# Cached keys of later groups turned by VectorE and moved by DMAs that ScalarE issues; the first sequence's tokens held twice

## The chip, the core and the metric

The kernel runs on one core of a Trainium2 chip. The core has a matrix engine (PE, with its weight loads shown as PEld), a vector engine (DVE), an activation engine (ACT), a general engine (POOL) and a queue engine that only issues transfers (SP). The metric is the device time of one execution in microseconds: before the change a median of 3047.43 us over 3 runs (3047.22 to 3047.49).

## The reference

A decoder layer with the norm after each of its three blocks. `x` has 32 sequences of 64 tokens with 512 features, 2048 token rows in all.

```
x = layernorm(x + attn(x))         # 32 heads, 8 key/value groups, head size 128
x = layernorm(x + xattn(x, ctx))   # the same heads over a context of 64 tokens a sequence
x = layernorm(x + ffn(x))          # one 512 x 512 product and a low-rank correction
```

The change lies in the first block:

```
q, k, v = x @ wq.T, x @ wk.T, x @ wv.T
q, k    = apply_rope(q), apply_rope(k)            # one position for all tokens
k_full  = concatenate([k_cache[block_idx], k[0]]) # 512 cached keys, 64 of the first sequence
v_full  = concatenate([v_cache[block_idx], v[0]])
out     = softmax(q @ k_full.T / sqrt(128)) @ v_full;  attn = out @ wo.T
```

All 2048 tokens attend to the same 576 keys, of which the first sequence gives 64. The kernel doesn't rotate the queries: since one rotation holds for all, it turns the cached keys back by it instead, and scales the new keys.

## The kernel before

**Stages.** Three stages follow each other: the self-attention (about the first 1840 us), the keys and values of the context (some 200 us), and the cross-attention with the feed-forward block. Everything is in 32-bit floating point.

**Units.** The first stage runs over 128 units: 8 groups (`NKV`) of 16 units, a unit being one head (4 a group, `REP`) with one block of 512 tokens (4 blocks, `NTB`). Unit r of a group, r = 0 to 15, is block r // 4, head r % 4. In a unit, `scores` runs four times, for 128 tokens each: two matmuls of 288 keys into `s` (two buffers), the row maximum on DVE (`nmax`), the exponential on ACT into `p`, the division on DVE, and a transpose of 32 x 32 blocks on DVE (`turn`) into `T` (two buffers). `move` then brings `T` to the tile `pT` (two buffers, each for two units) by 16 transfers that SP issues. Two units later `values` multiplies `pT` by the values on PE: those of unit n run in unit n + 2, the first of them after the second `scores`. Between the scores stand the products of the queries (`q_`) and of the output projection (`w_`).

**Order.** In this stage the program writes the order on PE, DVE and ACT by hand; SP's order and POOL's come from a scheduler. All engines work through their own list in order. A unit takes 12 to 18 us.

**Keys.** While a group runs, the keys of the next are made in steps:
- r = 4, 5, 6, 8: `gather_keys` and `gather_values` fetch 128 cached rows each by indirect transfers from POOL into `kn` and `v`.
- r = 8: `new_keys` multiplies the tokens of the first sequence (`x64`, 64 columns) by the weights of the group. The keys (`pk`) come out turned already, as head features x tokens. The values (`pv`) are wanted on partitions 0 to 63 and once more on 64 to 127, so each of the four parts of the 512 features has two matmuls with the same 64 columns as stationary operand and different output halves. Both go into the bank `po1`; ACT evicts them into `kT` and `v`.
- r = 9: `rotate` turns the cached keys back on DVE (4 instructions) and POOL (2), from `kn` into `kr`.
- r = 10: `cached_keys` transposes `kr` on PE, four times 128 x 128 into the bank `po1`; ACT evicts it into `kT` in two instructions, which multiply by `SCALE`.

The first group's keys are made in the same way ahead of the first unit.

**Queues and counters.** Every plain transfer of the program, of SP as of ACT, has one of eight completion counters (DMAHW0 to 7), dealt out in the order in which the scheduler placed the transfers. A transfer is issued only when the earlier one on its counter has landed: the issuing engine waits for that, whatever the two transfers carry. SP issues the moves of `T`, the weights `wq` and `wo` and the token blocks `xT`; ACT issues 16 loads of `acc`, a pair `wk`, `wv` for each later group, and a few moves at the stage's two ends. At the end of r = 11 SP issues the four loads of the next group's `wq` and a block `xT` of 1 MB, ahead of that unit's 16 moves.

Lines that are spoken of: 312 all products of queries and projection, 559 the gathers, 594 to 598 `rotate`, 612 and 618 `new_keys`, 622 and 626 its evictions, 632 and 635 `cached_keys`, 651 scores, 656 maximum, 659 exponential, 677 `turn`, 689 `move`, 697 `values`, 110 and 230 the loads of `xT` and of weights, 552 those of `wk` and `wv`, 1127 the cross-attention's transpose on DVE.

Of the kernel before, what the change touches and what calls it, by code (L numbers as in the profile page):

```python
# [9 lines left out]
F32 = mybir.dt.float32  # L10
I32 = mybir.dt.int32
AF = mybir.ActivationFunctionType
ALU = mybir.AluOpType
# [3 lines left out]
P = 128  # L17
DIM = 512
NH, NKV, HD = 32, 8, 128
REP = NH // NKV  # L20
NT = 2048
SEQ = 64
TB = 512
NTB = NT // TB
TPB = TB // P
NC = DIM // P
# [5 lines left out]
SQ = 32  # L32
NQD = P // SQ
# [10 lines left out]
SHARED, NPC = 4, 9  # L44
# [4 lines left out]
SCALE = 1.0 / math.sqrt(HD)  # L49
# [3 lines left out]
def decoder_layer(  # L53
# [30 lines left out]
    nc = tc.nc  # L84
# [412 lines left out]
    later = []  # L497


    with ExitStack() as ph:  # L500
        kv = ph.enter_context(tc.tile_pool(name="kv", bufs=2))
        kc = ph.enter_context(tc.tile_pool(name="kc", bufs=1))
# [11 lines left out]
        NKT = NSEL // P  # L514
        blk = kc.tile([P, NKT], I32, name="blk")
        nc.sync.dma_start(out=blk, in_=block_idx)
        xTs = {0: token_room(0, "xT0")}
# [6 lines left out]
        cs = kc.tile([P, HD // 2], F32, name="cs")  # L524
        sn = kc.tile([P, HD // 2], F32, name="sn")
# [20 lines left out]
        rows_cur, kn_cur, kr_cur, wkv_cur, kTs, vs = {}, {}, {}, {}, {}, {}  # L546
# [51 lines left out]
            nc.vector.tensor_tensor(k4[:, :, :, 0], k4[:, :, :, 0], tmp, ALU.add)  # L598


        x64 = kc.tile([P, NC, SEQ], F32, name="x64")

        def new_keys(g):

            wk, wv = wkv_cur.pop(g)
            kTs[g] = kv.tile([P, NKEY], F32, tag="kT", name=f"kT{g}")
            new = bank([P, 1, TB], f"new{g}", "po1")[:, 0, :]
            pk, pv = new[:, :SEQ], new[:, P : 2 * P]  # L610
            for c in range(NC):
                nc.tensor.matmul(
                    pk, wk[:, c, :], x64[:, c, :], start=(c == 0), stop=(c == NC - 1),
                    skip_group_check=True,
                )
            for c in range(NC):
                for i in range(2):
                    nc.tensor.matmul(
                        pv[i * SEQ : (i + 1) * SEQ, :], x64[:, c, :], wv[:, c, :],
                        start=False, stop=(c == NC - 1), skip_group_check=True,  # L620
                    )
            nc.scalar.activation(
                kTs[g].rearrange("p (s b k) -> p s b k", s=2, k=SQ)[:, :, SHARED, :],
                pk.rearrange("p (s k) -> p s k", s=2), AF.Copy, scale=nrm2,
            )
            nc.scalar.copy(vs[g][:, NKT, :], pv)

        def cached_keys(g, tag="po1"):
            kr = kr_cur.pop(g)
            pt = bank([P, NKT, P], f"pkt{g}", tag)  # L630
            for t in range(NKT):
                nc.tensor.transpose(pt[:, t, :], kr[:, t, :], ident)
            dst = kTs[g].rearrange("p (s b k) -> p s b k", s=2, k=SQ)
            for r0, b0 in ((0, 0), (2, SHARED + 1)):
                nc.scalar.activation(
                    dst[:, :, b0 : b0 + NKT, :],
                    pt[:, :, r0 * SQ : (r0 + 2) * SQ].rearrange("p t (s k) -> p s t k", s=2),
                    AF.Copy, scale=SCALE,
                )

        units = [(g, tb, h) for g in range(NKV) for tb in range(NTB) for h in range(REP)]
        qTs, Ts, pTs, oTs, pos, ps_ = {}, {}, {}, {}, {}, {}

        def scores(n, i):


            g, tb, h = units[n]
            u = f"{g}_{tb}_{h}_{i}"
            s = sc.tile([P, 2, 512], F32, tag="sc", name=f"s{u}")
            for a in range(2):  # L650
                nc.tensor.matmul(  # L651
                    s[:, a, :HALF], qTs[n // REP][:, units[n][2], i * P : (i + 1) * P],
                    kTs[g][:, a * HALF : (a + 1) * HALF], start=True, stop=True,
                )
            nmax = small.tile([P, 1], F32, tag="nmax", name=f"nmax{u}")
            nc.vector.tensor_reduce(nmax, s[:, :, :HALF], AX.XY, ALU.max, negate=True)  # L656
            p = sb.tile([P, NKEY], F32, tag="p", name=f"p{u}", bufs=4)
            den = small.tile([P, 1], F32, tag="den", name=f"den{u}")
            nc.scalar.activation(  # L659
                p.rearrange("q (a k) -> q a k", a=2), s[:, :, :HALF], AF.Exp,  # L660
                bias=nmax, accum_out=den,
            )
            if i == 0:
                Ts[n] = sb.tile([P, NBK, TPB, SQ], F32, tag="T", name=f"T{g}_{tb}_{h}")
                flush()
            else:
                turn(n, i - 1)
            nc.vector.reciprocal(den, den)  # L668
            nc.vector.tensor_scalar(p, p, den, None, ALU.mult)  # L669
            ps_[n, i] = p  # L670
            if i == TPB - 1:
                turn(n, i)
# [123 lines left out]
        t = {i: big.tile([P, 2, HF], F32, tag=f"tx{i}", name=f"tx0_{i}") for i in range(1, 5)}  # L796
        for j in range(NKT):
            gather_keys(0, j)
        nc.gpsimd.tensor_copy(
            x64.rearrange("p c (j k) -> p c j k", j=TPB),  # L800
            xTs[0].rearrange("p c (j k) -> p c j k", j=TPB)[:, :, :, : SEQ // TPB],
        )
        nc.vector.tensor_tensor(t[1], q[0, 1], q[0, 0], sub)
        nc.vector.tensor_tensor(wq0[7], wq0[1], wq0[5], sub)
        nc.vector.tensor_tensor(wq0[5], wq0[5], wq0[4], ALU.add)
# [13 lines left out]
        c = first.c  # L819
# [9 lines left out]
        for j in range(NKT):  # L829
            gather_values(0, j)  # L830
        cached_keys(0, "s0")
        nc.vector.tensor_tensor(t[3], q[1, 1], q[0, 1], sub)
        nc.vector.tensor_tensor(t[4], q[1, 0], t[2], sub)
        tok[1] = token_sums(xTs[1], "tx1", nc.gpsimd)
# [27 lines left out]
        for n in range(N):  # L862
            b, h = divmod(n, REP)
            g, r = units[n][0], n % PER
            if r == REP and g + 1 < NKV:
                load_group(g + 1)
            if r in gathers and g + 1 < NKV:
                gather_keys(g + 1, gathers[r])
            if 0 < n <= PER:


                b2, j = divmod(n - 1, TPB)
                nc.scalar.dma_start(out=acc[b2][:, j, :], in_=rows(x, b2)[:, j, :])
            if r == 2 * REP and g + 1 < NKV:
                later.append(lambda g=g: new_keys(g + 1))
            if r == 2 * REP + 1 and g + 1 < NKV:
                rotate(g + 1)
                later.append(lambda g=g: cached_keys(g + 1))
            if n == N - REP:
                encT[0] = big.tile([P, NC, TB], F32, tag="qT", name="encT0", bufs=2)  # L880
                load_features(encT[0], encT_in, 0)
            steps = {0: "qwqw", 1: "qw q", 2: "wqwq", 3: "w qw"}[h]

            def step(place):
                if n < REP:

                    i = {(0, 0): 3, (0, 1): 7, (0, 3): 4}.get((n, place))
                    if i:
                        last_products(i)
                    elif (n, place) in ((0, 2), (1, 0), (1, 1), (1, 2), (1, 3), (2, 0), (2, 2)):  # L890
                        q_step(n)
                elif steps[place] == "q":
                    q_step(n)
                elif steps[place] == "w":
                    w_step(b - 2 if h < 2 else b - 1)
                flush()

            def spare_bank():

                if n % 2 == 0 and later:  # L900
                    later.pop(0)()

            scores(n, 0)
            step(0)
            spare_bank()
            scores(n, 1)
            if n - 1 in short:
                move(n - 1, (3,), nc.scalar)
            if n >= 2:
                values(n - 2, 0, 2 if n % 2 == 0 else 3)  # L910
            step(1)
            scores(n, 2)
            step(2)
            if r in gathers and g + 1 < NKV:
                gather_values(g + 1, gathers[r])
            scores(n, 3)
            if n >= 2:
                values(n - 2, 2 if n % 2 == 0 else 3, NKT)
                if n % 2:
                    shared_values(n - 2)  # L920
            step(3)
            spare_bank()
            if h == REP - 1:
                if b + 2 < NB:
                    g2, tb2, _ = units[(b + 2) * REP]
                    if tb2 == 0:
                        wq_cur[g2] = load_left(wqT[:, columns(g2)], f"wq{g2}", nc.gpsimd)
                    tok[b + 2] = token_sums(xTs.pop(b + 2), f"tx{g2}_{tb2}", nc.gpsimd)
                elif b + 2 == NB:
                    kvw[0] = load_kv_left(0, "wq")  # L930
                else:
                    encR[0] = token_sums(encT[0], "te0", nc.gpsimd)
            if h == REP - 1 and b + 3 < NB or n == 0:

                b2 = b + 3 if n else 2
                xTs[b2] = token_room(b2, f"xT{b2}")
                load_features(xTs[b2], xT_in, b2 % NTB)
            move(n, (0, 1, 2) if n in short else range(NQD))
# [512 lines left out]
```

## Time and profile before

The profiled execution took 3049.76 us by the device's own count; the span from its first to its last instruction is 3048.0 us. Busy times by stage, in us:

| stretch, us | PE | DVE | ACT | POOL | DMA share |
|---|---|---|---|---|---|
| 0 to 1840 (self-attention) | 1823.22 | 1418.08 | 538.49 | 487.17 | 0.46 |
| 1840 to 2040 (context) | 198.13 | 93.88 | 33.72 | 41.63 | 0.44 |
| 2040 to 3048 (cross-attention, feed-forward) | 993.04 | 688.15 | 211.57 | 418.11 | 0.19 |
| the span, 3048 | 3014.40 | 2200.11 | 783.78 | 946.90 | |

The granted clock of the matrix engine is 0.997 on the mean. The DMA share is the mean busy share of the core's 16 DMA engines. A row of the timeline gives the start, the length, the engine (with q: its queue), the line, the operation, what it writes and reads, and the count of instructions that were merged; in brackets the idle time of the engine ahead of it and what ended that. A matmul in 32 bits shows as two PE records, a transpose as one. In the view of waits a row names who waited, for what, the sum, the number of times and the longest. SP has no busy time: all it does is to wait and to issue.

### The profile page before, as it was taken

What the parts mean: (1) busy time and instruction counts of PE and PEld (TensorE: products, weight loads), DVE (VectorE), ACT (ScalarE), POOL (GpSimd) and SP (SyncE); (2) the same over time, 40 slices, a digit from 0 to 9 for tenths busy, and PEclk for the clock granted to TensorE, in tenths of its full rate; (3) what the DMA queues carried; (4) which work ended last, traced back from release to release, by engine and by line L of the source; (5) the groups of instructions that cost most, each with busy time, mean ns of one, the idle gap of its engine ahead of it and who ended that gap; (6) DMA issues with size and microseconds to landing.
All of it is one profiled execution on the core that took longest, in us unless ns stands there. A gap on an engine that the chain in (4) does not pass through costs nothing.

```text
span 3048.0 us, 42453 instructions
## 1 busy us (share of the span) xinstructions
PE 3014.4 (99%) x14848; PEld 2321.9 (76%) x14848; DVE 2200.1 (72%) x4069; ACT 783.8 (26%) x1892; POOL 946.9 (31%) x774
## 2 busy tenths in 40 slices
PE   8999999999999999999999999999999999999998
PEld 6677777777777777777777768998888888888875
DVE  7777787777777777777877763546666666666787
ACT  2323223223222222222332221111111111111233
POOL 4231321321321321321321223035544444444420
PEclk9999999999999999999999999999999999999999
DMA  5444444444444444444444354351121121121121
GB/s 171 129 130 129 110 115 126 109 113 126 108 114 129 105 121 124 108 123 119 106 126 108 87 133 141 115 160 56 49 63 56 49 65 55 50 67 52 52 61 42
DMA packets 214931, 304.97 MB, mean 100 GB/s; under 512 B 45888, under 2 KB 108864, under 8 KB 214720
## 3 DMA queue, kind: packets, MB, share of 16 engines
q1 hardware_dynamic: 200048, 286.90, 34.7%
q10 hardware_dynamic: 12624, 11.16, 1.3%
q0 software_dynamic: 2048, 4.20, 0.5%
q8 instruction: 120, 1.97, 0.3%
q14 instruction: 91, 0.75, 0.1%
HBM read 107.05 MB, written 20.97 MB: 42 GB/s over the span
## 4 chain that ended last, share of the span: by engine, by line
PE 94%; DVE 2%; SPq 1%; DMA 1%; issue 1%; ACT 1%; POOL 0%; ACTq 0%; DVEq 0%; POOLq 0%
PE po L697 16%; PE s L651 15%; PE sx L1091 2%; PE pox L1163 2%; PE w_2y L312 1%; PE q_3y L312 1%; PE w_0y L312 1%; PE w_3y L312 1%; PE q_2y L312 1%; PE qx_0y L312 1%; PE wx_0y L312 1%; PE wx_3y L312 1%; PE qx_2y L312 1%; PE qx_1y L312 1%; PE wx_1y L312 1%; PE w_1y L312 1%
## 5 line engine op out<-in xcount | busy, mean ns | idle before, releaser
L659 ACT ACTIVATE p<-s,nmax 128x576 f32<-128x576 f32 x512 | 379.1, 740 | 1250.0 <-DVE nmax L656 1233.2
L651 PE MATMUL s<-kT,qT 128*128 128x288 f32 x2048 | 578.0, 408 | 4.9 <-ACT p L659 4.2
L697 PE MATMUL po<-pT,v 128*128 128x512 f32 (+1 forms) x1280 | 552.7, 605 | 6.2 <-DMA pT<-T 4.5
L651 PEld LDWEIGHTS s<-kT,qT 128*128 128x128 f32 x2048 | 388.4, 191 | 108.2 <-issue 19.7
L656 DVE TENSOR_REDUCE nmax<-s 128x1 f32<-128x576 f32 x512 | 384.0, 750 | 62.9 <-PE s L651 62.9
L677 DVE STREAM_TRANSPOSE T<-p 128x576 f32<-128x576 f32 x512 | 394.1, 770 | 4.4
L697 PEld LDWEIGHTS po<-pT,v 128*128 128x128 f32 (+1 forms) x1280 | 214.4, 190 | 208.5 <-issue 182.3
L669 DVE TENSOR_SCALAR p<-p,den 128x576 f32<-128x576 f32 x512 | 316.1, 617 | 17.9
L668 DVE RECIPROCAL den<-den 128x1 f32<-128x1 f32 x512 | 83.9, 164 | 230.9 <-ACT p L659 221.3
L283 POOL TENSOR_TENSOR so<-oT,oT 128x512 f32<-128x512 f32 x32 | 40.7, 1272 | 551.2 <-ACT oT L720 533.9
L286 POOL TENSOR_TENSOR so<-oT 128x512 f32<-128x512 f32 x32 | 40.6, 1270 | 351.2 <-ACT oT L720 100.6
L283 POOL TENSOR_TENSOR sox<-oTx,oTx 128x512 f32<-128x512 f32 x32 | 40.5, 1266 | 296.8 <-ACT oTx L1182 216.0
L1182 ACT ACTIVATE oTx<-pox,bv 128x128 f32<-128x128 f32 x256 | 73.7, 486 | 117.6 <-PE pox L1163 117.6
L224 POOL TENSOR_TENSOR tx<-xT 128x512 f32<-128x512 f32 x31 | 39.6, 1278 | 206.2 <-PE q_3z L312 65.0
L659 ACT ACTIVATION_READ_ACCUMULATOR p<-s,nmax 128x1 f32 x512 | 98.7, 193 | 0.0
L1292 POOL TENSOR_TENSOR txx<-x1T 128x512 f32<-128x512 f32 x31 | 39.3, 1268 | 174.6 <-PE qx_3z L312 75.2
L1108 ACT ACTIVATE ex<-ex 128x512 f32<-128x512 f32 x64 | 40.4, 631 | 201.7 <-DVE ex L1107 201.7
L1184 DVE TENSOR_SCALAR oTx<-pox,bv 128x128 f32<-128x128 f32 x256 | 72.6, 422 | 8.5 <-PE pox L1163 8.5
L1091 PEld LDWEIGHTS sx<-kvx,qTx 128*64 128x64 f32 x2048 | 62.3, 138 | 10.6 <-issue 10.6
L720 ACT COPY oT<-po 128x512 f32<-128x512 f32 x128 | 68.3, 587 | 4.7 <-PE po L697 3.8
L1091 PE MATMUL sx<-kvx,qTx 128*64 128x64 f32 x2048 | 66.7, 224 | 0.0
L1163 PE MATMUL pox<-pTx,kvx 64*128 64x256 f32 x512 | 64.6, 389 | 0.7 <-DMA pTx<-Tx 0.7
(443 smaller groups left out, 5746.1 us busy)
## 6 DMA issues: line engine op xcount, KB each, us to landing
pT<-T SPq DMA_DIRECT2D x1016, 80.0 KB
pT<-T SPq DMA_DIRECT2D x1008, 64.0 KB
xT<-in_xT SPq DMA_DIRECT2D x31, 1024.0 KB
kvx<-kv SPq DMA_DIRECT2D x32, 512.0 KB
pTx<-Tx SPq DMA_DIRECT2D x256, 64.0 KB
kv<-c SPq DMA_DIRECT2D x30, 512.0 KB
wo<-in_woT SPq DMA_DIRECT2D x32, 256.0 KB
xwq<-in_xwq SPq DMA_DIRECT2D x32, 256.0 KB
```

The costliest lines, as they stand in the source:

```text
L283: nc.gpsimd.tensor_tensor(t[1], a[1, 0], a[1, 1], ALU.add)
L312: nc.tensor.matmul(self.banks[b][:, m, :], self.left[i][:, k, m * P : (m + 1) * P], self.right[i][:, k, :], start=(first and m + k == 0), ...
L651: nc.tensor.matmul(s[:, a, :HALF], qTs[n // REP][:, units[n][2], i * P : (i + 1) * P], kTs[g][:, a * HALF : (a + 1) * HALF], start=True, s ...
L656: nc.vector.tensor_reduce(nmax, s[:, :, :HALF], AX.XY, ALU.max, negate=True)
L659: nc.scalar.activation(p.rearrange("q (a k) -> q a k", a=2), s[:, :, :HALF], AF.Exp, bias=nmax, accum_out=den,)
L668: nc.vector.reciprocal(den, den)
L669: nc.vector.tensor_scalar(p, p, den, None, ALU.mult)
L677: nc.vector.transpose(Ts[n][:, :, i, :], ps_.pop((n, i)).rearrange("q (b k) -> q b k", k=SQ))
L697: nc.tensor.matmul(pos[n].rearrange("d (a q) -> d a q", a=NQD), vs[units[n][0]][rows, v, :], pTs[n // 2][rows, :, chunk, :], skip_group_ch ...
L1091: nc.tensor.matmul(s[b * SEQ : (b + 1) * SEQ, i * REP + h, :], qTs[n][:, h, pr * HF + c0 : pr * HF + c0 + SEQ], kvs[n][:, pr, 0, c0 : c0 + ...
L1163: nc.tensor.matmul(po[pr, b][:, i, :].rearrange("d (h a j) -> d h a j", h=REP, a=2), kvs[n][r, pr, 1, i * HD : (i + 1) * HD], pTs[n][r, :, ...
L1182: nc.scalar.activation(dst, src, AF.Identity, bias=bias)
```

## The change

Three edits:
- `x64` becomes the first half of `x128`, which holds the 64 tokens twice. POOL fills it by two copies in place of one. `new_keys` makes the values by one matmul for each part of the features, with 128 stationary columns, in place of two with 64.
- For the seven later groups `cached_keys` (r = 10) goes: four transposes on PE and two evictions on ACT. In its place `turn_keys` follows `rotate` in r = 9: one 32 x 32-block transpose on DVE of 128 x 512, from `kr` back into `kn`. Sixteen transfers of `kn` into `kT`, of 16 KB each in 128 pieces of 128 bytes, carry the blocks to their partitions. ACT issues them, one behind each exponential, in r = 10 to 13. The built program deals them counters of the same eight; the lists of SP and of POOL keep their order, apart from POOL's second copy.
- `SCALE` is no longer applied by the evictions; after the first group's keys, DVE multiplies the cosines and sines (`cs`, `sn`, 128 x 64 each) by it once.

```diff
-        x64 = kc.tile([P, NC, SEQ], F32, name="x64")
+        x128 = kc.tile([P, NC, 2 * SEQ], F32, name="x128")
+        x64 = x128[:, :, :SEQ]
...
             for c in range(NC):
-                for i in range(2):
-                    nc.tensor.matmul(
-                        pv[i * SEQ : (i + 1) * SEQ, :], x64[:, c, :], wv[:, c, :],
-                        start=False, stop=(c == NC - 1), skip_group_check=True,
-                    )
+                nc.tensor.matmul(
+                    pv, x128[:, c, :], wv[:, c, :],
+                    start=False, stop=(c == NC - 1), skip_group_check=True,
+                )
...
+        def turn_keys(g):
+
+            kn_cur[g] = kn_cur[g].rearrange("p t (r k) -> p t r k", k=SQ)
+            nc.vector.transpose(
+                kn_cur[g], kr_cur.pop(g).rearrange("p t (r k) -> p t r k", k=SQ)
+            )
+
+        def move_keys(g):
+
+
+            dst = kTs[g].rearrange("p (s b k) -> p s b k", s=2, k=SQ)
+            for a in range(NQD):
+                b0 = SHARED + 1 if a > 1 else 0
+                for r in range(NQD):
+                    key_moves.append(lambda a=a, b0=b0, r=r: nc.scalar.dma_start(
+                        out=dst[r * SQ : (r + 1) * SQ, a % 2, b0 : b0 + NKT, :],
+                        in_=kn_cur[g][a * SQ : (a + 1) * SQ, :, r, :],
+                    ))
+
+        key_moves = []
...
                 bias=nmax, accum_out=den,
             )
+            if key_moves:
+                key_moves.pop(0)()
...
-        nc.gpsimd.tensor_copy(
-            x64.rearrange("p c (j k) -> p c j k", j=TPB),
-            xTs[0].rearrange("p c (j k) -> p c j k", j=TPB)[:, :, :, : SEQ // TPB],
-        )
+        for i in range(2):
+            nc.gpsimd.tensor_copy(
+                x128[:, :, i * SEQ : (i + 1) * SEQ].rearrange("p c (j k) -> p c j k", j=TPB),
+                xTs[0].rearrange("p c (j k) -> p c j k", j=TPB)[:, :, :, : SEQ // TPB],
+            )
...
         cached_keys(0, "s0")
+
+        for w in (cs, sn):
+            nc.vector.tensor_scalar(w, w, SCALE, None, ALU.mult)
...
                 rotate(g + 1)
-                later.append(lambda g=g: cached_keys(g + 1))
+                turn_keys(g + 1)
+            if r == 2 * REP + 2 and g + 1 < NKV:
+                move_keys(g + 1)
```

## The prediction

> **What bounds the kernel now.** I read the engines' busy shares and the chain of waits first.
>
> ```profile
> PE 3014.4 (99%) x14848; PEld 2321.9 (76%) x14848; DVE 2200.1 (72%) x4069; ACT 783.8 (26%) x1892; POOL 946.9 (31%) x774
> PE 94%; DVE 2%; SPq 1%; DMA 1%; issue 1%; ACT 1%; POOL 0%; ACTq 0%; DVEq 0%; POOLq 0%
> ```
>
> PE sets the time: a microsecond taken from its list is gained, one that it waits is lost. The timeline of PE shows what the two edited steps take of it, here for the last group:
>
> ```profile
> 1483.16 1.00 PE L612 MATMUL new<-x,wk 128*128 128x64 f32 x8
> 1484.10 1.09 PE L618 MATMUL new<-wv,x 128*64 128x128 f32 x16
> 1485.12 1.24 PE L651 MATMUL s<-kT,qT 128*128 128x288 f32 x4
> ...
> 1513.19 0.60 PE L632 MATMUL pkt<-ident,kr 128*128 128x128 f32 x4
> 1513.63 1.14 PE L651 MATMUL s<-kT,qT 128*128 128x288 f32 x4
> ```
>
> From start to next start, the values of the new keys hold PE for 1.02 us, the transposes for 0.44.
>
> The change puts transfers on ACT, so I then asked what SP's moves wait for, from 150 to 1600 us:
>
> ```profile
> SPq L689 <- DVE T L677: 267.2, 81, 5.8
> SPq L689 <- DMA wk<-in_wkT: 33.5, 6, 5.9
> SPq L689 <- DMA xT<-in_xT: 23.1, 9, 4.2
> SPq L689 <- DMA acc<-in_x: 7.4, 2, 5.0
> ```
>
> The first row is the data. The others are loads that have nothing to do with `pT`; `wk` and `acc` are issued by ACT. That is the shared counter at work: a transfer of ACT holds SP for up to 5.9 us.
>
> Whether PE feels it depends on the slack of `pT`. SP's and PE's timelines at the end of r = 11 in the last group, and PE's rows at the same place in the first and the third group:
>
> ```profile
> 1525.83 10.53 SPq L689 DMA_DIRECT2D pT<-T  x16
> 1536.40 2.15 SPq L230 DMA_DIRECT2D wq<-in_wqT  x4
> 1538.65 0.41 SPq L110 DMA_DIRECT2D xT<-in_xT  x1
> 1539.15 23.86 SPq L689 DMA_DIRECT2D pT<-T  x29
> ...
> 1556.79 2.74 PE L697 MATMUL po<-pT,v 128*128 128x512 f32 x6
> ...
> 197.78 2.81 PE L697 MATMUL po<-pT,v 128*128 128x512 f32 x6 [0.64 <-DMA pT<-T]
> ...
> 651.41 2.81 PE L697 MATMUL po<-pT,v 128*128 128x512 f32 x6 [0.44 <-issue]
> ```
>
> SP runs without a gap from the moves of r = 10 (1525.83) through `wq` and `xT` to those of r = 11. By the trace's landing records `xT` is in at 1548.05, the last move of r = 11 at 1555.15, and PE takes them up at 1556.79. In the seven groups this distance is 0.5, 1.4, 0.3, 2.1, 1.5, 0.3 and 1.6 us; some 0.3 of it is the way from landing to matmul, and in two groups PE already waits. In r = 9, 10 and 12 it is 3.3 us or more. So the values that run in r = 13 are the tight place.
>
> **The change part by part.**
>
> *Transposes off PE.* Seven groups x 0.44 = 3.1 us gained. ACT loses two evictions (0.66 us a group), which nothing waited for but the next group.
>
> *Values by the whole array.* Of the 16 records of line 618 each is 64 ns behind the last (1.02 / 16); 128 columns with a full weight load run at 110 ns (0.44 / 4 in the transposes). Eight such: 0.88 us, a gain of 0.14 a group, 1.0 us for the seven later ones. Here a rule speaks against the edit: the Trainium skill, "TensorEngine Tiling (Array Packing)", section "Theoretical Speedup", lets operands of 64 columns run as two tiles at up to twice the speed. If the halves ran fully beside each other, 0.88 us before, the edit would bring nothing; one after the other (16 x 110 ns = 1.76) it would bring 0.88 a group. The row lies near the first end, and I take it. In the first group the weight loads of the transposes that follow wait 0.17 us for POOL's last rotation, so most of it is lost there.
>
> *DVE's transpose in r = 9.* No such row in this stage; the nearest is the 128x512 transpose of line 1127, 694 ns. It stands ahead of the unit's first maximum (1499.56), delays it by 0.7 us and waits for POOL's last rotation (1498.12 + 0.79 = 1498.91), which DVE's own (1499.22 + 0.42) outlasts. The fourth scores need the second exponential, over at 1504.09, and start at about 1505.69 (1504.72 + 0.97): 1.6 us of cover. Cost 0; with the cover gone 7 x 0.7 = 4.9.
>
> *Scaling of cosines and sines, second copy.* Two small instructions on DVE before 19 us, while it then waits for the first scores until 20.94; POOL's second copy (0.89) ends at 10.6, its next instruction starts at 11.81 on gathered keys. Cost 0.
>
> *ACT's sixteen transfers.* Issuing one from SBUF to SBUF takes ACT some 0.6 us (its moves at line 689: 601 ns). ACT sits idle for 1.2 us or more ahead of every exponential in these units of the last group: hidden. ACT's own counters: I matched each wait in the built program's list with the landing before the change. Two to four moves a group wait for another move of the same set, long landed; nearly all others for a transfer of SP that landed 3 to 10 us earlier. The exception is the third move in r = 12, whose counter belongs to a move queued behind `xT`: from 1.9 us before to 1.4 after the exponential's end. Delayed by SP's 2 us (below) it can hold ACT past the next exponential by a microsecond or two; the second scores of r = 13 need that one 3 us later. Cost 0, up to 2 x 7 = 14 if this cover fails.
>
> *SP behind ACT's transfers.* In r = 11, SP's eleventh or so move has the counter of ACT's second. In the last group the second exponential ends at 1531.78; issue 0.1 later and 2.1 us to land (moves of SP land 2.0 to 2.2 us after issue; pieces of 128 bytes aren't in the trace of before: bounds 1.9, nothing faster being there, and 3.0, the gathers' median) gives 1533.98. SP would have issued at 1532.60: held by 1.4 us, and `wq`, `xT` and the moves of r = 11 with it. Then, behind `xT`: before, the eighth move waits for its counter and nine are left to issue. With ACT's transfers dealt in between, it is the seventh: one more issue, 0.63 us. Per group, in us:
>
> | group | 1 | 2 | 3 | 4 | 5 | 6 | 7 |
> |---|---|---|---|---|---|---|---|
> | SP held in r = 11 | 2.6 | 1.9 | 0.7 | 1.9 | 1.7 | 1.9 | 1.4 |
> | with the extra issue | 3.2 | 2.5 | 1.3 | 2.5 | 2.3 | 2.5 | 2.0 |
> | slack less 0.3 | 0.2 | 1.1 | 0 | 1.8 | 1.2 | 0 | 1.3 |
> | PE waits longer by | 3.0 | 1.4 | 1.3 | 0.7 | 1.1 | 2.5 | 0.7 |
>
> Sum 10.7 us; with a landing of 1.9 it is 9.3, with 3.0 it is 17. In r = 11 to 13 SP is held besides by up to 2 us a unit, which r = 10 and 12 cover with 3.3 us or more.
>
> The second rule to weigh: the Trainium skill, "DMA: Bandwidth & Descriptors", section "Issuing engines are not separate DMA queues", says that issuing from several engines saves only the issuing engine's time. By it the issue on ACT spares SP 16 x 0.63 = 10 us a group and costs it nothing: stall 0, sum -4.1. Below nothing it can't go, since these transfers come on top of SP's. The rows of `wk` and `acc` show a loss all the same, not of bandwidth (DMA share 0.46) but of order; I go by them.
>
> Sum: -3.1 - 1.0 + 10.7 = +6.6, rounded to +7 since the first group's `wq` loads are held as well. Against the profiled execution, 3049.76 + 7 = 3056.8; it lies 2.3 above the median of the runs, so 3047.43 + 7 = **3054.5 us** is my forecast.
>
> **Rivals.**
> 1. *The holds stay hidden* (0.28). If SP makes up what it loses before r = 13, only PE's 4.1 us count: 3043.3. For it: SP idles 4 to 5 us ahead of the moves of r = 8, 9 and 10. Against: no idle time from 1525.83 to `xT`. This case isn't slower.
> 2. *ACT is held too* (0.15). The third move of r = 12 delays exponentials, PE runs out of scores: +7 from above and half of the 14: 3061.5. It decides once such a wait ends over 3 us behind its exponential.
> 3. *The halves ran one after the other* (0.07), with the holds hidden: 7 x (0.44 + 0.88) = 9.2 gained, 3038.2. Against it stands 64 ns a record.
>
> My own case has 0.50. A difference under 0.2% (6.1 us) is about what this measurement can tell from no change. The main case spreads from +3 to +14, mostly above 6.1: 0.40 slower, 0.10 within. With rival 2 slower has 0.55; rival 1 adds 0.27 within and 0.01 faster, rival 3 0.07 faster: within 0.37, faster 0.08. Range for eight in ten: 3042.5 (rival 1 with a little more) to 3063 (a landing of 3.0, or ACT held).
>
> **What would show it.** In the changed profile: lines 632 and 635 only at the start; line 619 taking 0.88 us; SP's waits listing `kT<-kn` some ten times a group; PE's idle time before line 720 (the values) with some 11 us more, in r = 13. If that idle time stays near 6 us, rival 1 holds. If PE's scores wait for ACT, rival 2. If line 619 takes 0.5 us, the rate of 110 ns was wrong.

## The result, and the profile after

The changed kernel takes 3066.19 us, the median of 6 runs (3061.64 to 3068.97), the kernel before beside it 3047.32 (3045.55 to 3049.19, 6 runs). The ratio is 1.0063, with a 95% interval of 1.0053 to 1.0073: **slower by 18.9 us**. The profiled execution took 3064.98 us, 15.2 more than the profiled one of before; the one of before lies 2.4 us above its median beside it, the one of after 1.2 below.

The page of the changed kernel: PE's busy time, the chain of waits, and the group of the values (busy time and mean ns, then PE's idle time ahead of it and what ended most of that), with the last row of before under it.

```profile
PE 3013.8 (98%) x14756; PEld 2319.0 (76%) x14756; DVE 2200.5 (72%) x4078; ACT 778.7 (25%) x1878; POOL 947.2 (31%) x775
...
PE 88%; DVE 4%; DMA 3%; SPq 3%; ACT 1%; issue 1%; POOL 0%; ACTq 0%; DVEq 0%; POOLq 0%
...
L720 PE MATMUL po<-pT,v 128*128 128x512 f32 (+1 forms) x1280 | 553.6, 606 | 16.1 <-DMA pT<-T 15.7
```
```profile
L697 PE MATMUL po<-pT,v 128*128 128x512 f32 (+1 forms) x1280 | 552.7, 605 | 6.2 <-DMA pT<-T 4.5
```

PE's list is shorter by 92 matmuls, yet it is busy for only 0.6 us less, and the chain leaves it far more often (88% for 94). The idle time ahead of the values grew from 6.2 to 16.1 us. From 150 to 1620 us, SP's waits, then PE's, then PE's of before (who waits for what: sum, times, longest):

```profile
SPq L712 <- DMA kT<-kn: 49.1, 21, 7.6
...
SPq L712 <- DMA xT<-in_xT: 4.6, 5, 2.1
...
SPq L230 <- DMA acc<-in_x: 2.7, 1, 2.7
```
```profile
PE po L720 <- DMA pT<-T: 11.1, 6, 2.3
PE q_0x L312 <- DMA wq<-in_wqT: 4.9, 6, 2.8
```
```profile
PE po L697 <- DMA pT<-T: 0.6, 1, 0.6
PE q_0x L312 <- DMA wq<-in_wqT: 0.2, 1, 0.2
```

SP now stands 49 us behind moves of keys, which it has no use for. Where: the queue of SP and the timeline of ACT at the end of r = 11 and in r = 12 of the last group.

```profile
1552.44 2.15 SPq L230 DMA_DIRECT2D wq<-in_wqT  x4
1554.69 0.41 SPq L110 DMA_DIRECT2D xT<-in_xT  x1
```
```profile
1556.28 0.74 ACT L680 ACTIVATE p<-s,nmax 128x576 f32<-128x576 f32 x1 [2.62 <-DVE nmax L677]
1556.33 0.60 ACTq L656 DMA_DIRECT2D kT<-kn  x1
...
1559.35 0.59 ACTq L656 DMA_DIRECT2D kT<-kn  x1
```

Two things are to be read here. ACT issues a move 0.05 us after the exponential ahead of it has begun, not after it has ended. And the two moves of 1556.33 and 1559.35 go out while the 1 MB of `xT` is in flight. By the landing records `xT` is in at 1563.39, the two moves at 1564.2 and 1564.4, 7.9 and 5.0 us after their issue (in groups 2 to 7: 7.9 to 9.1 and 4.8 to 6.1), where the moves of r = 10 and 11 take 2.0 in the median. SP's fourth move of r = 11 has the counter of the first of them. From 1555 to 1580 us SP's waits are one row; under it the row of before for the same place (1539 to 1564 us):

```profile
SPq L712 <- DMA kT<-kn: 6.0, 1, 6.0
```
```profile
SPq L689 <- DMA xT<-in_xT: 3.2, 1, 3.2
```

Before, the eighth move of r = 11 was the first to wait, for `xT` itself, and nine were left to issue once it was in; now it is the fourth, and thirteen are left. In r = 13 PE waits for these moves before it can take up the values: in each of groups 2 to 7, by 1.35 to 2.27 us.

A wait can cost more than its own length. PE's timeline at two such waits, in the sixth group and in the third, and the windows around the first (busy us of PE, PEld, DVE, ACT and POOL, then the granted clock, the DMA share and GB/s):

```profile
1344.82 4.51 PE L720 MATMUL po<-pT,v 128*128 128x512 f32 x6 [2.07 <-DMA pT<-T]
```
```profile
659.46 2.84 PE L720 MATMUL po<-pT,v 128*128 128x512 f32 x6 [2.27 <-DMA pT<-T]
```
```profile
1340.00:1345.00 5.00, 2.93 (x14) 2.19 (x13) 2.80 (x6) 1.66 (x4) 0.00 (x0) 1.00 0.51 122
1345.00:1350.00 5.00, 5.00 (x10) 2.38 (x10) 1.25 (x3) 0.00 (x0) 0.00 (x0) 0.66 0.51 121
```

Behind the first the granted clock is 0.66 in the mean of 5 us and the same six records take 4.51 us, not 2.84. Behind the second, though it is the longer wait, they take no longer.

### The profile page after: what moved, and what is told of

Its sections match the earlier page's. It is cut to its first block, busy times and chain, and to the rows that moved or that the text cites. A ratio compares the mean times of both kernels' runs of the same rounds, so it can differ in the third digit from the quotient of the medians.

```text
span 3063.2 us, 42403 instructions
## 1 busy us (share of the span) xinstructions
PE 3013.8 (98%) x14756; PEld 2319.0 (76%) x14756; DVE 2200.5 (72%) x4078; ACT 778.7 (25%) x1878; POOL 947.2 (31%) x775
## 4 chain that ended last, share of the span: by engine, by line
PE 88%; DVE 4%; DMA 3%; SPq 3%; ACT 1%; issue 1%; POOL 0%; ACTq 0%; DVEq 0%; POOLq 0%
PE po L720 15%; PE s L672 14%; SPq L712 2%; PE sx L1120 2%; PE pox L1192 2%; DMA kT<-kn 2%; PE w_0y L312 1%; PE q_2y L312 1%; PE w_3y L312 1%; PE qx_0y L312 1%; PE wx_0y L312 1%; PE wx_3y L312 1%; PE w_2y L312 1%; PE qx_2y L312 1%; PE qx_1y L312 1%; PE wx_1y L312 1%
## 5 line engine op out<-in xcount | busy, mean ns | idle before, releaser
L720 PE MATMUL po<-pT,v 128*128 128x512 f32 (+1 forms) x1280 | 553.6, 606 | 16.1 <-DMA pT<-T 15.7
```

Source lines behind the costliest of these rows:

```text
L720: nc.tensor.matmul(pos[n].rearrange("d (a q) -> d a q", a=NQD), vs[units[n][0]][rows, v, :], pTs[n // 2][rows, :, chunk, :], skip_group_ch ...
```

## The experiments

**My theory** after the two traces (A in the expectations): ACT's moves cost nothing themselves; they hold SP through the shared counters, and PE feels it where SP's own transfers have no slack, above all behind `xT` in r = 12. Against it stood, in the first four runs, two others (B and C there): that the transfers in pieces of 128 bytes take it from the other transfers, and that DVE's transpose delays the maxima. Each run below stands against the kernel before, timed beside it with a median of 3046.0 to 3046.2 us.

**1. The values alone.** The kernel before, with only the edit of `x128`.

```diff
-                for i in range(2):
-                    nc.tensor.matmul(
-                        pv[i * SEQ : (i + 1) * SEQ, :], x64[:, c, :], wv[:, c, :],
+                nc.tensor.matmul(
+                    pv, x128[:, c, :], wv[:, c, :],
```

> Only the first edit: the 64 tokens twice, values of the new keys by the whole array; cached keys as before. In the changed profile the step from the first matmul of the new keys to the next scores is 1.79 us against 1.96, so every theory expects 7 x 0.17 = 1.2 us less than before (3047.3 to about 3046.1), and no wait of SP on anything new. If it costs several us instead, part of the loss is in this edit.

Measured 3047.33 us, ratio 1.0 (0.9992 to 1.0009). The interval is 2.7 us to either side, so a gain of this size can't be told from none by the time. It can in the trace. PE's timeline of the last group:

```profile
1479.14 1.00 PE L613 MATMUL new<-x,wk 128*128 128x64 f32 x8
1479.98 1.11 PE L618 MATMUL new<-wv,x 128*128 128x128 f32 x8
1480.93 1.14 PE L651 MATMUL s<-kT,qT 128*128 128x288 f32 x4
```

From start to start the values take 0.95 us (before 1.02), the keys ahead of them 0.84 (0.94), and the scores behind them last 1.14 (1.24). Together 0.27 us: in each of the seven groups the unit r = 8, from its first exponential to the next unit's, is 0.27 to 0.28 us shorter.

**2. No move behind `xT`.** The change, with two moves behind each exponential, so that all sixteen are out in r = 10 and 11.

```diff
-            if key_moves:
+            for _ in range(min(2, len(key_moves))):
```

> The changed kernel, but two key moves behind each exponential, so that all sixteen are issued in r = 10 and 11 and none while the 1 MB load of tokens is in flight (r = 12). Theory A (SP is held by the completion counter of a key move that lands only behind that load): the idle time of PE before the values of r = 13 falls from 11 us to 2 or less, time 3043 to 3047. Theory B (the 14336 extra pieces of 128 bytes crowd the DMA engines, whatever the counters): the same pieces are moved, so 3060 or more. Theory C (DVE's transpose and ACT's issues delay the scores): the same instructions, 3060 or more.

Measured 3061.12 us, ratio 1.0049 (1.0036 to 1.0062). A miss of the expectation in time. SP's and PE's waits, again from 150 to 1620 us:

```profile
SPq L712 <- DMA kT<-kn: 26.4, 24, 2.1
```
```profile
PE q_0x L312 <- DMA wq<-in_wqT: 11.8, 6, 3.3
```

The wait for `pT` in r = 13 is gone, as A says; but SP, held in r = 10 and 11 by moves just issued, comes to the `wq` loads late, and PE waits 1.5 to 3.3 us a group in r = 12. There are thus two tight places, not one. A second reading was open: that the sixteen moves cost the same wherever they stand.

**3. The same transfers from another engine.** The change, with POOL issuing the moves. POOL's transfers don't share the eight counters.

```diff
-                    key_moves.append(lambda a=a, b0=b0, r=r: nc.scalar.dma_start(
+                    key_moves.append(lambda a=a, b0=b0, r=r: nc.gpsimd.dma_start(
```

> The changed kernel with the key moves issued by POOL, whose transfers have counters of their own; r = 10 to 13 as in the changed kernel, subject to POOL's order. Theory A: SP waits for no key move, the idle time before the values of r = 13 goes back to about 1 us, time 3043 to 3050 (POOL has 16 issues of about 1 us more a group, which may delay its sums for the projection). Theory B: the same pieces in flight with the token load, 3060 or more. Theory C: 3060 or more, since DVE's transpose is there still.

Measured 3046.43 us, ratio 1.0001 (0.9993 to 1.0009). The edit changed more than the engine: POOL's order comes from the scheduler, which put all sixteen moves straight behind DVE's transpose. POOL's timeline in the last group, whose r = 10 begins at 1516.01:

```profile
1503.61 9.11 POOL L656 DMA_DIRECT2D kT<-kn  x16 [1.84 <-DVE kn L645]
```

So they go out in r = 9, in every group, and none stands beside `wq` or `xT`. SP waits for no `kT<-kn` at all, and PE's waits are small:

```profile
PE q_0x L312 <- DMA wq<-in_wqT: 2.7, 2, 1.4
PE po L720 <- DMA pT<-T: 2.1, 2, 1.3
```

DVE's transpose is there, and the loss isn't: C falls as its cause. On B this run alone doesn't decide, since the pieces of 128 bytes don't meet `xT`. Against B speak the landings of the changed kernel: in groups 2 to 7 the `xT` of r = 12 lands 8.7 to 10.3 us after its issue (before 8.5 to 11.1), and the moves of `T` in 2.07 us in the median, as before. The other transfers aren't slower.

**4. The moves without the rest.** The kernel before, with sixteen moves a group of the gathered keys into a tile that nothing reads, issued by ACT as in the change.

```diff
+        spare = kc.tile([P, NKEY], F32, name="spare")
...
+            if r == 2 * REP + 2 and g + 1 < NKV:
+                move_keys(g + 1)
```

> The kernel before with sixteen moves of the gathered keys into a spare tile that nothing reads, issued by ACT in r = 10 to 13 as the changed kernel's are; transposes on PE and halves as before, no transpose on DVE. Theories A and B: the loss without the gains, 3047.3 + 18.9 + 5 = about 3071, SP waiting on the moves as in the changed kernel. Theory C without DVE's part: 3047 to 3052.

Measured 3065.12 us, ratio 1.0055 (1.0043 to 1.0067): 19.0 us by the medians, 6 less than the 3071 expected. A loss of that size is there without any other part of the change:

```profile
SPq L705 <- DMA spare<-kn: 47.9, 19, 7.2
```
```profile
PE po L713 <- DMA pT<-T: 13.3, 7, 2.8
```

**5 and 6. The place of the moves.** The change, with two moves behind each exponential of r = 13 and 14, where no `wq` is waiting to be issued and `xT` is in; and, as the counterpart, of r = 12 and 13.

```diff
-            if key_moves:
+            for _ in range(min(2, len(key_moves))):
...
-            if r == 2 * REP + 2 and g + 1 < NKV:
+            if r == 3 * REP + 1 and g + 1 < NKV:
```

The second has `3 * REP` there. From here on B stands for the reading that experiment 2 left open: every move costs SP about the same, wherever it stands.

> The whole change, but its sixteen moves of ACT are set two behind each exponential of r = 13 and 14, after the group's wq and xT loads have landed and while no load of 1 MB is in flight. Theory A (SP is held through the shared counters, and it costs only where SP's own transfers have no slack: the wq loads of r = 11, and everything behind xT in r = 12 and 13): SP's waits still list kT<-kn, each under 3 us, PE's waits for wq and pT go back to those of the kernel before, and the 0.7 us a group that PE saves remains: 3043 us (3041 to 3046). Theory B (each move of ACT costs SP about the same wherever it stands; taking it from r = 12 only shifts the loss, as the run with all moves in r = 10 and 11 did): the loss appears as PE's wait for pT in r = 14 and 15 or for wq in r = 0, 3055 to 3062 us.

> The same with the moves two behind each exponential of r = 12 and 13, so that the first of them are issued while xT is still in flight. Theory A: those land only behind xT, 5 to 9 us after their issue as the two of the changed kernel did, SP's moves of r = 12 are held by them, and PE's waits for pT in r = 13 become longer than the changed kernel's 11.1 us: 3066 to 3076 us; where such a wait passes 2.5 us, the granted clock falls for some microseconds behind it. Theory B: as with r = 13 and 14, 3055 to 3062 us. If the wq loads of r = 11 were what counts, they are issued before all moves here and the run would be near 3045 us.

In r = 13 and 14: **3044.34 us** (3042.11 to 3050.79), ratio 0.9997 (0.9988 to 1.0005). PE's busy time on its page, and SP's and PE's waits:

```profile
PE 3008.7 (99%) x14756; PEld 2319.0 (76%) x14756; DVE 2200.8 (72%) x4078; ACT 779.5 (26%) x1878; POOL 947.4 (31%) x775
```
```profile
SPq L712 <- DMA kT<-kn: 30.9, 37, 3.1
```
```profile
PE po L720 <- DMA pT<-T: 0.3, 1, 0.3
PE po L720 <- issue: 0.2, 1, 0.2
PE q_0x L312 <- DMA wq<-in_wqT: 0.2, 1, 0.2
```

SP is still held by ACT's moves, 31 us in all and up to 3.1 at a time; PE waits 0.7 us in all. So a hold alone costs nothing: it is the place, and with it the later transfer that gets the counter. A new place deals the counters anew, and no run parts the two. In r = 12 and 13: 3065.79 us, ratio 1.0062 (1.0048 to 1.0076), 0.2 under the range that A gives. Of PE's four waits over 2.5 us only the one of 3.0 was followed by a lower clock, where A expected all.

```profile
PE po L720 <- DMA pT<-T: 14.9, 6, 2.8
PE po L720 <- DMA kT<-kn: 3.0, 1, 3.0
PE q_0x L312 <- DMA wq<-in_wqT: 0.3, 1, 0.3
```

The two kernels differ by one unit in the place of sixteen moves, and by 21 us. The reading B falls.

**7. POOL, meant for r = 13 and 14.** As experiment 5, with `nc.gpsimd`.

> The moves issued by POOL, two behind each exponential of r = 13 and 14. With r = 10 to 13 POOL's moves held no move of SP, but PE still waited 2.7 us for wq in r = 12 in two groups, and the 0.7 us a group did not show in the median. Theory A: here nothing stands near the wq loads, PE's waits are those of the kernel before and the saving shows: 3042 us (3040 to 3045). Theory D (POOL's issuing, or the transfers themselves, take back the 0.7 us a group wherever they stand): 3046 us, as before.

Measured 3046.18 us, ratio 1.0001 (0.9992 to 1.0009): the number of D, not of A. But here too POOL issues all sixteen moves in r = 9 (in the last group from 1499.57 on for 9.11 us; r = 10 begins at 1511.96). The run repeats experiment 3 and says nothing of r = 13 and 14. PE still waits 3.4 us for `wq` in three groups and 1.1 us for `pT`. SP waits for no move of keys, so what makes `wq` late in these groups, here and in experiment 3, isn't the hold by keys. I didn't find it; since POOL's moves are dealt no counter of the eight, SP's own transfers are dealt others than before, but that this is the reason is only argued.

**8. SP in r = 13 and 14.** As experiment 5, with `nc.sync`. In SP's order, which is the scheduler's, the moves go out in r = 13 to 15.

> The moves issued by SP itself, two behind each exponential of r = 13 and 14, in its own order and with its own counters. Theory A: nothing of ACT holds SP, but it issues sixteen more transfers at some 0.6 us, 5 us a unit against 3.3 to 5 us of slack there: 3043 to 3050 us, with PE waiting for pT in r = 14 or 15 by up to 1 us a group. Theory B (the count of transfers on SP's list is what costs, whoever issues them): as much as the changed kernel, 3060 us or more.

Measured 3049.42 us, ratio 1.0011 (1.0004 to 1.0018). PE waits 5.0 us for `pT`, mainly at the head of the next group. Sixteen more issues on SP's list cost 3 us, a sixth of what the shared counters cost in the changed kernel.

**9. Only the moves of r = 12 elsewhere.** The change, with its moves in r = 10, 11, 13 and 14. This parts the step of the prediction (a hold in r = 11) from the one that the trace suggests (moves queued behind `xT`).

```diff
-            if key_moves:
+            if key_moves and n % (NTB * REP) != 3 * REP:
```

> The changed kernel with its moves one behind each exponential in r = 10, 11, 13 and 14: the four of r = 12, of which the first two land only behind xT, are the only ones that change places. If what holds SP is above all the moves queued behind xT (as the trace of the changed kernel suggests), PE's waits for pT in r = 13 go from 11.1 us to under 3, its waits for wq in r = 12 stay near 5 us, and the time is 3049 us (3046 to 3052). If instead the hold in r = 11, before wq and xT are issued, carries the loss to r = 13, as the prediction had it, PE still waits 7 us or more for pT in r = 13 and the time is 3056 us or more. Theory B (each of ACT's moves costs about the same wherever it stands): as the changed kernel, 3060 us or more; it would contradict the run with r = 13 and 14.

Measured 3048.46 us, ratio 1.0009 (1.0002 to 1.0015).

```profile
SPq L712 <- DMA kT<-kn: 8.5, 14, 1.7
```
```profile
PE q_0x L312 <- DMA wq<-in_wqT: 4.0, 5, 2.6
PE po L720 <- DMA pT<-T: 1.2, 2, 0.7
```

The eight moves of r = 10 and 11 stay, and with them PE's wait for `wq` (4.0, in the changed kernel 4.9). The wait for `pT` goes from 11.1 to 1.2 us. The loss goes from 6.3 to 0.9 in a thousand, so some 16.5 of the 18.9 us hang on the place of the four moves of r = 12.

No version beats the kernel before by what can be measured. The best, experiment 5, lies 1.8 us below it, inside its interval.

## Why the prediction was wrong

The direction was right, and the kind of mechanism: a transfer of ACT holds SP by a shared counter, and PE pays in r = 13. Which hold does it was wrong, and the size was too small: +7 (3054.43, given as 3054.5) for 18.9, above all because two terms were put at nothing. By the profiled executions (15.2), in us; the right column is PE's waits of after less those of before, for the gain the length of the units r = 8 to 11, and for the clock 1.7 us (half of 3.41) for each of two stretches at half the clock:

| term | predicted | measured |
|---|---|---|
| transposes and values, 7 groups | -4.1 | -4.9 |
| values wait for `pT` in r = 13 | +10.7 | +10.5 |
| queries wait for `wq` in r = 12 | 0 | +4.7 |
| PE at a lower granted clock, groups 1 and 6 | 0 | +3.4 |
| sum | +6.6 | +13.7 |

The units r = 8 to 13 of the seven groups are 15.4 us longer, 1.7 more than this sum. PE's busy time around the waits is up to 0.24 us a unit longer where the clock is full; why isn't shown. The rest of the execution comes out even only by chance. After loses 1.9 us more before 110 us. Before loses 2.8 more in the last group, where it waits 3.1 us for `pT` at 1792 and then runs at half the clock for 6.8 us. The later stages add 0.7. Over the whole execution, up to the end of PE's work, both kernels had half the clock for the same 13.7 us, so the term of the clock belongs to these two groups of this trace and isn't a fixed price of the change.

*Transposes off PE, values by the whole array.* Right in kind. The seven groups gain 0.70 us each in place of 0.58. Experiment 1 shows that the values bring 0.27 and not 0.14, since the rows on either side also become shorter. The 110 ns for a matmul of 128 columns were 119 (0.95 / 8), not far from two of the halves' 64. So the edit gains little. That fits the rule on tiles, two halves beside each other; but the weight loads of the halves are shorter too (137 ns for 192), and no run parts the two.

*DVE's transpose in r = 9* and *ACT's issues cost ACT nothing.* Right. The group of scores has 4.9 us of idle time ahead of it before and after; the delay that the transpose brings at the head of r = 9 is made good by the end of r = 11.

*SP behind ACT's transfers.* This is the step that failed, in three of its terms. That the sum in r = 13 came out right is chance: group 1, for which 3.0 us were forecast, doesn't wait there at all, and groups 2 to 7 wait 11.1 us for 7.7.
- The hold in r = 11 was sized at 0.7 to 2.6 us a group, from an issue "0.1 later" than the exponential's end. The moves are issued 0.05 us after its start, 0.7 us sooner, and in groups 2 to 7 this hold is 0 to 0.6 us (in group 1 1.1).
- The landing of 2.1 us was taken for every move. It is right (2.0) for those of r = 10 and 11, and the pieces of 128 bytes cost nothing more. It is wrong for the first two of r = 12, which in groups 2 to 7 land 4.8 to 9.1 us after issue, 0.5 to 1.0 us behind `xT`. The trace of before had it already: SP's own first seven moves of r = 11, issued behind `xT` from 1539.15 to 1544.21, land from 1548.21 to 1549.28, 5.1 to 9.1 us after issue. The prediction saw that the *third* of r = 12 depends on a move behind `xT`, and asked only what ACT would lose by it.
- "One more issue" was four more. In groups 2 to 7 SP stops at its fourth move of r = 11 for 6 to 7.6 us and has thirteen to issue afterwards: 4 x 0.63 = 2.5 us later. Experiment 9, which keeps the moves of r = 10 and 11, shows that this, not the hold in r = 11, is the wait for `pT`; experiment 6 shows it from the other side.

*The `wq` loads* got only a rounding, from 6.6 to 7, and cost 4.7: the second step that failed, a term put at nothing. SP comes to them later by what r = 10 and 11 hold it; in group 1 one of them also waits 2.7 us for a load of `acc`, by the new dealing of counters, and PE 2.8. Experiment 2 shows what this place can cost, 11.8 us of waits. *The clock behind a wait*, the other term at nothing, cost 3.4.

*The rivals.* The first (the holds stay hidden) is what experiment 5 makes true by moving the moves; in the change they don't. The second (ACT held too) didn't happen: PE waits for ACT as before. The third falls with the 119 ns.

*The rule on issuing engines* (by it the stall would be 0) holds for the transfers themselves: issued by POOL, in r = 9, they cost nothing that can be measured, and issued by SP 3 us. It says nothing of what the issuing engine must wait for before it issues, and that is where the 19 us are.

*What would show it.* Lines 632 and 635 only at the start, PE's idle time ahead of the values 9.9 us longer (some 11 foreseen): as said. SP's waits list `kT<-kn` about three times a group, not ten, but with 2.3 us each.

## What to carry to other kernels

A transfer added on an idle engine isn't free if its completion counter is shared: look up which later transfer of the busy queue waits for it, and when it will have landed *there*, behind what is then in flight. Put such transfers where the busy queue has slack and no large load is under way; here one unit's distance was worth 21 us. Check in the built program's trace where a transfer really went out before reading a result from its place. And before costing a wait of PE of about 2 us at its length, look at the granted clock behind such waits in the same trace.

## What the runs showed of the hardware

**PE's clock is halved behind 3.41 us in which PE did little.** In ten of the eleven traces (not in experiment 8) the granted clock falls to one half amid PE's work, for 3.41 or 6.83 us at a time, and these stretches begin on one grid of 3.41 us. I divided all traces along that grid, from 30 us on. Every piece at full clock with PE busy for up to 1.44 us was followed by half the clock; of those with 1.48 to 1.73 us some were; none with more was. (Ends of matmuls are modelled, so these times are rough.) What counts is thus how a wait lies on the grid. Two pieces around a wait of 2.07 us in the changed kernel, then two around one of 2.82 us in experiment 6 (PE's busy time stands first behind the length, the clock third from the end):

```profile
1341.79:1345.20 3.41, 1.34 (x5) 0.70 (x5) 2.24 (x5) 0.83 (x2) 0.00 (x0) 1.00 0.52 124
1345.20:1348.61 3.41, 3.41 (x5) 1.35 (x4) 1.05 (x3) 0.00 (x0) 0.00 (x0) 0.50 0.51 121
```
```profile
1110.83:1114.24 3.41, 2.07 (x10) 1.38 (x8) 2.41 (x6) 0.83 (x2) 0.00 (x0) 1.00 0.57 131
1114.24:1117.65 3.41, 1.94 (x5) 1.01 (x6) 1.87 (x4) 0.83 (x2) 0.00 (x0) 1.00 0.64 146
```

The shorter wait lies within one piece; the longer is shared by two. That is why in the first stage beyond 150 us seven of the fifteen waits between 2.07 and 2.82 us lowered the clock, and all three of 3.0 us or more. In the changed kernel the waits of 2.81 and 2.07 us cost 1.7 us each beyond themselves; in experiment 4 one of 2.73 us cost 2.7 (six records of the values in 5.46 us, for 2.74). The Trainium skill, "TensorE: Matmul & The Clock Gate", Part 1, has a free-running window of about 3.4 us, and half the clock after an idle one. The grid agrees. That the window needn't be idle throughout (PE was busy for 0.60 to 1.73 us in those that lowered the clock amid the work) is not in its rule, and the measurement decides.

**An issue doesn't wait for the activation ahead of it.** Of the 112 moves that stand behind exponentials in ACT's list in the changed kernel, 98 go out 0.05 us after the exponential's start (1556.33 against 1556.28), 0.7 us before its end. They read nothing that it writes.

**A small move behind a large load lands after it.** 16 KB from SBUF to SBUF land in 2.0 us, but with 1 MB of SP's queue in flight in 4.8 to 9.1, in each of groups 2 to 7 0.5 to 1.0 us after the load. In the last group the move of 1556.33 has its first packet at 1560.1, and its completion comes at 1564.2, behind that of the load (1563.39).
